# The last pair of a graph layer: inverse root on GpSimd, totals and turn-back in one PSUM slot, value copies on ScalarE

## The chip, the cores and the metric

The kernel runs on one core of a Trainium2 chip. The metric is the device time of one execution in microseconds (us); before the change three runs gave a median of 4974.71 us (4970.81 to 4975.93). In the profile PE is TensorE, DVE VectorE, ACT ScalarE, POOL GpSimd, SP the queue that issues all transfers. Everything is fp32, and each fp32 product shows as two matrix instructions in the trace (a transpose as one).

## What is computed

Two graph attention layers over 4096 nodes with 512 features and 8 heads of 64. Each normalizes its rows, takes the positive part, and adds attention to the input:

```python
h = jnp.maximum(_layernorm(x, axis=-1), 0.0)
x = x + _L0_gnn_ref(h, adj, L0_gnn_W, L0_gnn_b, L0_gnn_src_proj, L0_gnn_trg_proj)
h = jnp.maximum(_layernorm(x, axis=-1), 0.0)
x = x + _L1_gnn_ref(h, adj, L1_gnn_Wks, L1_gnn_Wqs, L1_gnn_Wvs, L1_gnn_Wo)

# layer 0, per head
e = src.T[:, :, None] + trg.T[:, None, :]
e = jnp.where(e >= 0, e, 0.01 * e) + connectivity[None, :, :]
out = jnp.einsum('hnm,hmd->hnd', jax.nn.softmax(e, axis=-1), data1.transpose(1, 0, 2))

# _layernorm
(x - m) / jnp.sqrt(v + eps)
```

Layer 1 needs keys, queries and values of the normalized output of layer 0 (`h @ Wks`, `h @ Wqs`, `h @ Wvs`).

## The kernel before

Layer 0 treats its four pairs of heads one after another. The first three take about 1715 us and are not touched. The fourth pair has a stage of its own (its pools are called `b0...`), in which the rows of layer 0 become complete, and which therefore also normalizes them and makes layer 1's keys, queries and values. Layer 1 follows from about 2530 us on and isn't touched.

**Tiling.** A row block is 128 rows, 32 of them in the stage (NG). A row block has four steps (GS): a step is 32 rows, laid on 128 partitions as four column ranges of 1024, for both heads. So the stage has 128 steps (SETS), and eight steps make a norm block of two row blocks (BR). All intermediate tiles of a row block stay in a ring of 12 slots (RING), that is three row blocks.

**Order.** The order is written out by hand in the loop at the end of the stage, under a manual schedule: each engine does what the loop records for it, in that order, and waits where a result or a buffer isn't there yet. In step s:

- SP: the mask loads for step s+3 (L586).
- ACT: for the first step of a row block, `out_of_psum` of the row block before (boT, L665); then `leaky` of step s+1 (two of 128x1024 into PSUM, L599), `exps` of step s-3 (two of 128x1024, L641). The two PSUM tiles `lk` are all there is, so `leaky` of step s+1 waits for `masked` of step s.
- DVE: `masked` of step s (two of 128x1024, L609, with the row's minimum), `squares` of step s-4 (a transpose in 32x32 squares, 128x2048, L648).
- POOL: at odd s `parted` (L616), the minima spread for a product.
- `work()`: up to six units of a projection job (below).
- At even s `smallest`: PE brings the minima of two steps together (nmB, L625), DVE takes them (L630); `exps` needs them.
- `endings`: one more piece of each running `finish` (below), the oldest first.
- PE: `weighted` of step s-8, a quarter of the products of a row block (32 instructions, L656). With the fourth quarter, a new `finish` begins.

**finish.** It is a generator that goes on by one piece per step. After the step with the fourth quarter, before the change: in the second step PE sums the totals (den, L672) and DVE takes their reciprocal (L676). In the fourth PE turns the attention back (back, L680), DVE divides (L682), POOL adds it to the rows (L686), SP writes them (L687). In the fifth DVE takes the moments (L690, L694). For the second row block of a norm block it goes on: in the sixth ACT takes the root (L700), in the seventh DVE the reciprocal (L702) and POOL normalizes both row blocks (L706), in the ninth and tenth PE transposes one of them each (tp, L716) and DVE takes the positive part out of PSUM (bhT, L717). Then a projection job is queued.

**Projection job.** 48 units per norm block: 32 for keys and queries in four tiles (mp, L727), each copied out by ACT (L733), and 16 for values in two tiles (mpv, L739), each copied out by DVE (L745). SP writes them to DRAM (L734, L746). Eight steps with six units are 48 units, so one job just fills the time until the next.

**PSUM slots.** Two slots with the tag `mp` are shared by mp, mpv and tp. One slot with the tag `ms` is shared by nmB, den and back. Root and exponential belong to different tables of ACT; the program loads a table where they alternate (the rows ACT_TABLE_LOAD).

Of the kernel before, what the change touches and what calls it, by code (L numbers as in the profile page):

```python
# [8 lines left out]
F32 = mybir.dt.float32  # L9
AF = mybir.ActivationFunctionType  # L10
ALU = mybir.AluOpType
# [4 lines left out]
P = 128  # L16
EPS = 1e-5
# [6 lines left out]
def kernel(  # L24
# [14 lines left out]
    nc = tc.nc  # L39
    N, DM = x.shape  # L40
    H, D = src_proj.shape[1:]
# [9 lines left out]
    const = ctx.enter_context(tc.tile_pool(name="const", bufs=1))  # L51
    dram = ctx.enter_context(tc.tile_pool(name="dram", bufs=1, space=DRAM))

    ident = const.tile([P, P], F32, name="ident")
    make_identity(nc, ident)
    eps = const.tile([P, 1], F32, name="eps")
    nc.gpsimd.memset(eps, EPS)


    SQ = 32  # L60
    NS = P // SQ
    band = const.tile([P, SQ], F32, name="band")
# [36 lines left out]
    with tc.tile_pool(name="a0k", bufs=1) as pk, tc.tile_pool(name="a0v", bufs=4) as pv, tc.tile_pool(  # L99
        name="a0a", bufs=3  # L100
    ) as pa, tc.tile_pool(name="a0t", bufs=6) as pt, tc.tile_pool(name="a0p", bufs=4) as pp, tc.tile_pool(
        name="a0x", bufs=1
    ) as px, tc.tile_pool(name="a0h", bufs=3) as ph, tc.tile_pool(name="a0s", bufs=4) as psb, tc.tile_pool(
        name="a0tr", bufs=3, space=PSUM
# [112 lines left out]
        def finish(G):  # L217

            rows, cols = bass.ts(G.g, P), bass.ts(G.c, PR)
            after = bass.ts(G.c + 1, PR)  # L220
            xt = px.tile([P, PR], F32, name="xt")
            nc.sync.dma_start(xt, x[rows, cols])
            oT = px.tile([P, P], F32, name="oT")
            nc.vector.tensor_copy(oT, G.o[:, :P])
            den = psb.tile([P, 2], F32, name="den")
            nc.vector.reciprocal(den, G.sm)
            yield
            back = G.o[:, P : 2 * P]
            nc.tensor.transpose(back, oT, ident)
            for i in range(len(G.blocks)):  # L230
                for kc in range(KC):
                    nc.tensor.matmul(
                        G.o[:, bass.ts(2 + i, P)], lhsT=G.hT[i][:, kc, :], rhs=wt[:, kc, after],
                        start=(kc == 0), stop=(kc == KC - 1),
                    )
            yield
            att = px.tile([P, 2, D], F32, name="att")
            nc.vector.tensor_mul(
                att, back.rearrange("p (h d) -> p h d", d=D), den.unsqueeze(2).to_broadcast([P, 2, D])
            )  # L240
            nc.gpsimd.tensor_add(xt, xt, att.rearrange("p h d -> p (h d)"))
            for i, b in enumerate(G.blocks):
                d1 = px.tile([P, PR], F32, name="d1")
                nc.vector.tensor_add(d1, G.o[:, bass.ts(2 + i, P)], bb[:, after])
                nc.sync.dma_start(d1_d[bass.ts(b, P), after], d1)
            nc.sync.dma_start(x1_d[rows, cols], xt)
# [178 lines left out]
        def step(n):  # L425
            return groups[n // 2], n % 2

        with tc.manual_schedule():
# [45 lines left out]
            for s in range(total + 6):  # L474
                G, h = step(s) if s < total else (None, 0)
                for half in range(2):
# [31 lines left out]
                    if 1 <= n <= 2 * total:  # L508
                        W, w = groups[(n - 1) // HALVES], (n - 1) % HALVES
                        weighted(W, w)  # L510
                        if w == 0:
                            load_rows_turned(W)
                        if W.g == NB - 1 and W.c + 1 < PAIRS:
                            load_feats(W.c + 1, w)
                        if w == HALVES - 1:
                            endings = [*endings[-1:], finish(W)]
# [12 lines left out]
    BR = 2  # L529
    UNITS = 6  # L530
    with tc.tile_pool(name="b0c", bufs=1) as pc, tc.tile_pool(name="b0a", bufs=4) as pa, tc.tile_pool(
        name="b0w", bufs=1
    ) as pk, tc.tile_pool(name="b0t", bufs=1) as pt, tc.tile_pool(name="b0v", bufs=GS) as pv, tc.tile_pool(
        name="b0x", bufs=6
    ) as pxr, tc.tile_pool(name="b0h", bufs=4) as ph, tc.tile_pool(name="b0e", bufs=4) as pe, tc.tile_pool(
        name="b0ht", bufs=2
    ) as phT, tc.tile_pool(
        name="b0s", bufs=6
    ) as psb, tc.tile_pool(name="b0o", bufs=1) as px, tc.tile_pool(
        name="b0lk", bufs=2, space=PSUM  # L540
    ) as plk, tc.tile_pool(name="b0m", bufs=1, space=PSUM) as pm, tc.tile_pool(
        name="b0po", bufs=1, space=PSUM
# [124 lines left out]
        def finish(G):  # L667

            yield
            den = pm.tile([P, P], F32, tag="ms", name="den")  # L670
            for k in range(GS):
                nc.tensor.matmul(  # L672
                    den[bass.ts(k, SQ), :2], lhsT=band, rhs=G.sm[:, k, :], start=True, stop=True
                )
            rden = psb.tile([P, 2], F32, name="rden")
            nc.vector.reciprocal(rden, den[:, :2])  # L676
            yield
            yield
            back = pm.tile([P, P], F32, tag="ms", name="back")
            nc.tensor.transpose(back, G.oT, ident)  # L680
            att = px.tile([P, 2, D], F32, name="batt")
            nc.vector.tensor_mul(  # L682
                att, back.rearrange("p (h d) -> p h d", d=D), rden.unsqueeze(2).to_broadcast([P, 2, D])
            )
            last = G.x[:, C3 * PR :]
            nc.gpsimd.tensor_add(last, last, att.rearrange("p h d -> p (h d)"))  # L686
            nc.sync.dma_start(x1_d[bass.ts(G.g, P), C3 * PR :], last)  # L687
            yield
            stats = psb.tile([P, 6], F32, name="bstats")
            nc.vector.bn_stats(stats, G.x)  # L690
            if G.g % BR == 0:
                block[0] = psb.tile([P, BR, 2], F32, name="bmv")
            mv = block[0]
            nc.vector.bn_aggr(mv[:, G.g % BR], stats)  # L694
            if G.g % BR < BR - 1:
                return
            Gs = groups[G.g - BR + 1 : G.g + 1]
            yield
            rstd = psb.tile([P, BR, 1], F32, name="brstd")
            nc.scalar.activation(rstd, mv[:, :, 1:2], AF.Sqrt, bias=eps)  # L700
            yield
            nc.vector.reciprocal(rstd, rstd)  # L702
            hns = []
            for j in range(BR):
                hn = ph.tile([P, DM], F32, name="bhn")
                nc.gpsimd.tensor_scalar(  # L706
                    hn, Gs[j].x, mv[:, j, 0:1], rstd[:, j], ALU.subtract, ALU.mult
                )
                hns.append(hn)
            yield  # L710
            hT = phT.tile([P, KC, BR * P], F32, name="bhT")
            for j in range(BR):
                yield
                tp = pmm.tile([P, KC, P], F32, tag="mp", name="tp")
                for kc in range(KC):
                    nc.tensor.transpose(tp[:, kc, :], hns[j][:, bass.ts(kc, P)], ident)  # L716
                nc.vector.tensor_scalar(hT[:, :, bass.ts(j, P)], tp, 0.0, None, ALU.max)  # L717
            jobs.append(projected(Gs, hT))

        def projected(Gs, hT):  # L720

            rows = bass.ts(Gs[0].g // BR, BR * P)
            for c in range(HC):
                mp = pmm.tile([P, 2, BR * P], F32, tag="mp", name="mp")
                for i, w in ((0, wk), (1, wq)):
                    for kc in range(KC):
                        nc.tensor.matmul(  # L727
                            mp[:, i], lhsT=w[:, kc, bass.ts(c, P)], rhs=hT[:, kc, :],
                            start=(kc == 0), stop=(kc == KC - 1),
                        )  # L730
                        if (i, kc) == (1, KC - 1):
                            e = pe.tile([P, 2, BR * P], F32, name="e")
                            nc.scalar.copy(e, mp)  # L733
                            nc.sync.dma_start(qk_d[:, c, :, rows], e)  # L734
                        yield 1
            for j in range(BR):
                mp = pmm.tile([P, 512], F32, tag="mp", name="mpv")
                for kc in range(KC):
                    nc.tensor.matmul(  # L739
                        mp, lhsT=hT[:, kc, bass.ts(j, P)], rhs=wv[:, kc, :],  # L740
                        start=(kc == 0), stop=(kc == KC - 1),
                    )
                    if kc == KC - 1:
                        e = pe.tile([P, 512], F32, name="e")
                        nc.vector.tensor_copy(e, mp)  # L745
                        nc.sync.dma_start(v_d[bass.ts(Gs[j].g, P), :], e)  # L746
                    yield 2

# [16 lines left out]
        with tc.manual_schedule():  # L765
# [4 lines left out]
            for s in range(SETS + PROD + 10):  # L770
# [23 lines left out]
                if s % 2 and s < SETS:  # L794
                    G, k = step(s)
# [3 lines left out]
                if s % 2 == 0 and 0 <= s - 2 < SETS:  # L799
                    G, k = step(s - 2)  # L800
# [3 lines left out]
                if 0 <= n < SETS:  # L804
                    W, w = step(n)
                    weighted(W, w)
                    if w == GS - 1:
                        endings = [*endings[-2:], finish(W)]
# [21 lines left out]
    with tc.tile_pool(name="a1t", bufs=1) as pt, tc.tile_pool(name="a1k", bufs=4) as pkk, tc.tile_pool(  # L830
        name="a1v", bufs=GS
    ) as pv, tc.tile_pool(name="a1a", bufs=6) as pa, tc.tile_pool(name="a1q", bufs=2) as pq, tc.tile_pool(
        name="a1x", bufs=2
    ) as px, tc.tile_pool(name="a1s", bufs=6) as psb, tc.tile_pool(name="a1z", bufs=2) as pz, tc.tile_pool(name="a1at", bufs=3) as pat, tc.tile_pool(
        name="a1sc", bufs=4, space=PSUM
    ) as psc, tc.tile_pool(name="a1tr", bufs=1, space=PSUM) as ptr, tc.tile_pool(
        name="a1m", bufs=2, space=PSUM
# [263 lines left out]
        with tc.manual_schedule():  # L1101
# [18 lines left out]
            for s in range(total + PROD + 3):  # L1120
# [16 lines left out]
                if s % 2 and 0 <= s - 3 < total:  # L1137
                    G, k = step(s - 3)
                    smallest(G, k // 2)
                n = s - PROD  # L1140
                if 0 < n <= total and n % GS == 0:
                    finish(groups[n // GS - 1])
# [12 lines left out]
                if s % 2 and s < total:  # L1155
                    G, k = step(s)
# [16 lines left out]
            for j in range(rb, NB):  # L1173
                projected(j)
# [28 lines left out]
```

## Time and profile before

| what | value |
|---|---|
| median of three runs | 4974.71 us (4970.81 to 4975.93) |
| profiled execution, its own time | 4974.76 us |
| its span, first to last instruction | 4973.0 us, mean clock 0.978 |
| busy: PE, DVE, ACT, POOL | 4747.3, 4509.1, 3912.2, 396.1 us |
| the last pair of layer 0 | about 1715 to 2530 us |
| ACT_TABLE_LOAD at L700 and L641 | 15 and 14, 1283 ns each |
| L700, root on ACT | 16, 296 ns each |
| L706, norm on POOL (subtract, multiply) | 32, 2073 ns each |
| L338, norm on POOL in an earlier stage (multiply, add) | 32, 768 ns each |
| L745, value copy on DVE | 32, 670 ns each |
| L733, key and query copy on ACT | 64, 566 ns each |

How to read it: a row names the line, the engine, the operation and the tiles (output <- input, partitions x elements). Matrix instructions are pipelined, so their mean is not their distance. The share of busy time is a mean over a stage; waits show who stood still for whom, and where a wait was for several things, the trace names the one that came last, which need not be the one that was late.

### The profile page before, as it was taken

How to read it: one execution, taken by the hardware profiler on the slowest of the kernel's cores; microseconds unless marked ns; L12 is line 12 of the kernel's file. 1: busy time of each engine (PE TensorE's matmuls, PEld its weight loads, DVE VectorE, ACT ScalarE, POOL GpSimd, SP SyncE). 2: the span in 40 equal slices, each digit the busy share in tenths (PEclk: the TensorE clock that was granted, in tenths of full speed). 3: DMA queues.
4: the chain of work that ended last, by engine and by line, in shares of the span. 5: the costliest groups of instructions: out<-in, count | busy, mean ns of one | idle time of the engine just before them, and what ended most of it. 6: DMA issues, size and time to landing. Idle time of an engine off the chain costs nothing.

```text
span 4973.0 us, 145263 instructions
## 1 busy us (share of the span) xinstructions
PE 4747.3 (95%) x61554; PEld 3507.7 (71%) x61554; DVE 4509.1 (91%) x7969; ACT 3912.2 (79%) x4557; POOL 396.1 (8%) x676
## 2 busy tenths in 40 slices
PE   6999999999999868998989999999999999999998
PEld 5888888888888756776746656666666666666664
DVE  4999999999999898888659999999999999999981
ACT  4999999999999898888658888666666666666660
POOL 1000000000000011111112222000000000000000
PEclk8999999999999979999999999999999999999999
DMA  6444454445444474444377787634444343533435
GB/s 236 156 150 162 171 183 154 157 154 197 165 147 163 121 170 141 134 143 141 100 217 242 239 261 239 200 129 144 137 160 152 128 153 127 187 128 136 152 121 191
DMA packets 358842, 819.49 MB, mean 165 GB/s; under 512 B 60080, under 2 KB 179120, under 8 KB 333104
## 3 DMA queue, kind: packets, MB, share of 16 engines
q1 hardware_dynamic: 358192, 810.21, 49.8%
q8 instruction: 483, 7.91, 0.7%
q14 instruction: 167, 1.37, 0.1%
HBM read 669.26 MB, written 140.77 MB: 163 GB/s over the span
## 4 chain that ended last, share of the span: by engine, by line
PE 42%; DMA 3%; issue 2%; SPq 1%; ACT 1%; DVE 1%; POOL 0%; ACTq 0%; POOLq 0%; DVEq 0%
PE sc L915 17%; PE o L996 17%; PE tr L979 5%; PE oo L1079 2%; DMA a<-in_adj_dram 2%; ACT t L966 1%; PE nmB L950 1%; SPq L889 1%; POOL a L902 0%; DVE t L931 0%; PE mp L727 0%; DMA z<-inv_d 0%; PE mpv L739 0%; DMA att_d<-z 0%; DMA v<-v_d 0%
## 5 line engine op out<-in xcount | busy, mean ns | idle before, releaser
L931 DVE CUSTOM_DVE_ANT_0 t<-sc,a 128x512 f32<-128x512 f32 x2048 | 1291.3, 686 | 70.8 <-issue 41.2
L966 ACT ACTIVATE t<-t,nm 128x1024 f32<-128x1024 f32 x1024 | 1168.0, 1143 | 177.3 <-DVE nm L955 177.3
L996 PEld LDWEIGHTS o<-t,v 128*64 128x64 f32 x16384 | 884.6, 137 | 428.7 <-issue 363.1
L915 PE MATMUL sc<-k,q 64*32 64x512 f32 x16384 | 1004.0, 597 | 10.6 <-DVE nm L931 10.5
L996 PE MATMUL o<-t,v 128*64 128x128 f32 x16384 | 1008.3, 276 | 0.0
L973 DVE STREAM_TRANSPOSE t<-t 128x1536 f32<-128x1536 f32 x512 | 907.7, 1773 | 5.0 <-ACT t L966 2.0
L158 DVE CUSTOM_DVE_ANT_0 t<-t,a 128x2048 f32<-128x2048 f32 x384 | 877.0, 2284 | 38.8 <-ACT t L147 38.7
L181 PE MATMUL tr<-ident,t 128*128 128x128 f32 x6144 | 781.4, 278 | 34.0 <-ACT pT L190 20.1
L203 PE MATMUL o<-pT,v 128*64 128x128 f32 x12288 | 756.9, 276 | 1.1 <-DVE pT L192 1.0
L181 PEld LDWEIGHTS tr<-ident,t 128*128 128x128 f32 x6144 | 665.4, 141 | 125.8 <-issue 65.3
L147 ACT ACTIVATE t<-tb,src 128x4096 f32<-128x4096 f32 x192 | 731.6, 3811 | 16.8 <-DMA tb<-trg_d 16.8
L168 ACT ACTIVATE t<-t,nm 128x4096 f32<-128x4096 f32 x192 | 731.2, 3808 | 8.6 <-DVE nm L163 8.5
L203 PEld LDWEIGHTS o<-pT,v 128*64 128x64 f32 x12288 | 664.1, 137 | 61.4 <-issue 47.4
L192 DVE COPY pT<-tr 128x1024 f32<-128x1024 f32 x549 | 653.6, 1216 | 9.8 <-PE tr L181 9.8
L985 ACT COPY t<-tr 128x512 f32<-128x512 f32 x512 | 298.9, 584 | 445.6 <-PE tr L979 441.8
L915 PEld LDWEIGHTS sc<-k,q 64*32 64x32 f32 x16384 | 251.3, 106 | 351.6 <-issue 314.4
L979 PE MATMUL tr<-ident,t 128*128 128x128 f32 x2048 | 348.5, 288 | 11.6 <-ACT t L966 8.4
L599 ACT ACTIVATE lk<-tb,srcb 128x1024 f32<-128x1024 f32 x256 | 282.3, 1113 | 82.3 <-DVE nm L609 75.2
L609 DVE CUSTOM_DVE_ANT_0 bt<-lk,ba 128x1024 f32<-128x1024 f32 x256 | 301.9, 1215 | 24.8 <-ACT e L733 12.7
L648 DVE STREAM_TRANSPOSE bt<-bt 128x2048 f32<-128x2048 f32 x128 | 295.1, 2306 | 28.9 <-ACT bt L641 28.9
L979 PEld LDWEIGHTS tr<-ident,t 128*128 128x128 f32 x2048 | 213.9, 141 | 116.1 <-issue 83.1
L641 ACT ACTIVATE bt<-bt,nm 128x1024 f32<-128x1024 f32 x256 | 290.3, 1135 | 0.4 <-DVE nm L630 0.3
(115 smaller groups left out, 3781.7 us busy)
## 6 DMA issues: line engine op xcount, KB each, us to landing
a<-in_adj_dram SPq DMA_DIRECT2D x192, 1024.0 KB
a<-pen_d SPq DMA_DIRECT2D x384, 512.0 KB
ba<-in_adj_dram SPq DMA_DIRECT2D x512, 128.0 KB
a<-in_adj_dram SPq DMA_DIRECT2D x512, 128.0 KB
pen_d<-a SPq DMA_DIRECT2D x128, 512.0 KB
h<-hT_d SPq DMA_DIRECT2D x96, 256.0 KB
qk_d<-e SPq DMA_DIRECT2D x64, 256.0 KB
x<-in_x_dram SPq DMA_DIRECT2D x8, 1024.0 KB
```

The source lines that it names most:

```text
L147: nc.scalar.activation(t, targets[G.c, h], AF.Prelu, bias=src[:, G.g, 2 * G.c + h : 2 * G.c + h + 1], alpha=SLOPE)
L158: nc.vector.tensor_tensor_reduce(out=t, in0=t, in1=rows_of_adj[G, f], scale=-1.0, scalar=FMAX, op0=ALU.add, op1=ALU.min, accum_out=nm[:, f ...
L168: nc.scalar.activation(G.t[h], G.t[h], AF.Exp, bias=G.nm[h][:, NCH : NCH + 1], scale=-1.0, accum_out=G.sm[:, h : h + 1],)
L181: nc.tensor.transpose(tr[:, bass.ts(b % 4 * 2 + h, P)], G.t[h][:, bass.ts(i * MB + b, P)], ident)
L192: nc.vector.tensor_copy(pT, tr)
L203: nc.tensor.matmul(G.o[h * D : (h + 1) * D, :P], lhsT=feats[G.c][i][:, b, bass.ts(h, D)], rhs=pT[:, bass.ts(b % 4 * 2 + h, P)], start=(mb ...
L915: nc.tensor.matmul(sc[h][bass.ts(a, SQ), :], lhsT=G.q[bass.ts(h, D), bass.ds(G.q0 + k * SQ, SQ)], rhs=keys[G.c][half][bass.ts(h, D), a, :] ...
L931: nc.vector.tensor_tensor_reduce(out=t[:, G.ring + k, h, cols], in0=scs[half][h], in1=a[:, cols], scale=1.0, scalar=FMAX, op0=ALU.add, op1 ...
L966: nc.scalar.activation(u, u, AF.Exp, bias=G.nm[k // 2][:, k % 2, h : h + 1], scale=-1.0, accum_out=G.sm[:, h, k : k + 1],)
L973: nc.vector.transpose(u, u)
L979: nc.tensor.transpose(tr[:, bass.ts(h * NT + m, P)], t[:, G.ring + k, h, bass.ds(VC + m * P, P)], ident)
L996: nc.tensor.matmul(G.o[bass.ts(h, D), :P], lhsT=v[:, b, bass.ts(h, D)], rhs=t[:, bass.ds(G.ring, GS), h, bass.ds(at, SQ)], start=(mb == 0) ...
```

## The change

In the stage of the last pair:

- ACT's root and DVE's reciprocal are replaced by POOL: add epsilon, raise to the power -0.5, multiply by the mean, negate. The norm itself becomes a multiply-add with two values per row.
- The totals and the turn-back of a row block share one tile in the `ms` slot, and are done in the same piece of `finish`; the pieces after it follow sooner, so that a job is queued seven steps after the fourth quarter instead of ten.
- The value copies go from DVE to ACT, where they follow `exps` of the step.

Line numbers after the first edit are two higher in the changed kernel, and others shift by a few more.

```diff
+    neghalf = const.tile([P, 1], F32, name="neghalf")
+    nc.gpsimd.memset(neghalf, -0.5)
...
         def finish(G):
 
             yield
-            den = pm.tile([P, P], F32, tag="ms", name="den")
+            ms = pm.tile([P, 2, P], F32, tag="ms", name="back")
             for k in range(GS):
                 nc.tensor.matmul(
-                    den[bass.ts(k, SQ), :2], lhsT=band, rhs=G.sm[:, k, :], start=True, stop=True
-                )
+                    ms[bass.ts(k, SQ), 1, :2], lhsT=band, rhs=G.sm[:, k, :], start=True, stop=True
+                )
+            nc.tensor.transpose(ms[:, 0], G.oT, ident)
             rden = psb.tile([P, 2], F32, name="rden")
-            nc.vector.reciprocal(rden, den[:, :2])
-            yield
-            yield
-            back = pm.tile([P, P], F32, tag="ms", name="back")
-            nc.tensor.transpose(back, G.oT, ident)
+            nc.vector.reciprocal(rden, ms[:, 1, :2])
             att = px.tile([P, 2, D], F32, name="batt")
             nc.vector.tensor_mul(
-                att, back.rearrange("p (h d) -> p h d", d=D), rden.unsqueeze(2).to_broadcast([P, 2, D])
+                att, ms[:, 0].rearrange("p (h d) -> p h d", d=D), rden.unsqueeze(2).to_broadcast([P, 2, D])
             )
...
             if G.g % BR < BR - 1:
                 return
             Gs = groups[G.g - BR + 1 : G.g + 1]
-            yield
+
             rstd = psb.tile([P, BR, 1], F32, name="brstd")
-            nc.scalar.activation(rstd, mv[:, :, 1:2], AF.Sqrt, bias=eps)
-            yield
-            nc.vector.reciprocal(rstd, rstd)
+            nc.gpsimd.tensor_scalar(rstd, mv[:, :, 1:2], 1.0, EPS, ALU.mult, ALU.add)
+            nc.gpsimd.tensor_tensor(rstd, rstd, neghalf.unsqueeze(1).to_broadcast([P, BR, 1]), ALU.pow)
+            shift = psb.tile([P, BR, 1], F32, name="bshift")
+            nc.gpsimd.tensor_mul(shift, mv[:, :, 0:1], rstd)
+            nc.gpsimd.tensor_scalar(shift, shift, -1.0, 0.0, ALU.mult, ALU.add)
             hns = []
             for j in range(BR):
                 hn = ph.tile([P, DM], F32, name="bhn")
-                nc.gpsimd.tensor_scalar(
-                    hn, Gs[j].x, mv[:, j, 0:1], rstd[:, j], ALU.subtract, ALU.mult
-                )
+                nc.gpsimd.tensor_scalar(hn, Gs[j].x, rstd[:, j], shift[:, j], ALU.mult, ALU.add)
                 hns.append(hn)
+            yield
             yield
...
                     if kc == KC - 1:
                         e = pe.tile([P, 512], F32, name="e")
-                        nc.vector.tensor_copy(e, mp)
+                        nc.scalar.copy(e, mp)
                         nc.sync.dma_start(v_d[bass.ts(Gs[j].g, P), :], e)
```

## Prediction

> **What bounds the kernel now.** I first cut the span into stretches. Layer 0's last pair, the only stage that the diff touches, runs from about 1715 to 2530 us; the rest of the 4973.0 us keeps its code. Its two parts, with busy time per engine (PE, weight loads, DVE, ACT, POOL):
>
> ```profile
> core 0: us, PE busy (x) PEld busy (x) DVE busy (x) ACT busy (x) POOL busy (x), PEclk, DMA share, GB/s
> 1870.00:2437.00 567.00, 515.27 (x4486) 403.42 (x4485) 501.10 (x693) 498.18 (x697) 75.18 (x100) 0.93 0.47 136
> 2437.00:2530.00 93.00, 89.84 (x598) 64.35 (x604) 24.50 (x42) 17.17 (x30) 10.70 (x9) 1.00 0.30 104
> ```
>
> In the loop PE, DVE and ACT are all near 90%: none is the bound alone, they wait for each other. The ending is PE alone. The waits from 1870 to 2430 us say where (total, times, longest):
>
> ```profile
> ACT lk L599 <- DVE nm L609: 65.7, 48, 2.3
> PEld mpv L739 <- ACT e L733: 45.7, 12, 3.8
> DVE bt L648 <- ACT bt L641: 25.2, 12, 2.1
> PE tp L716 <- DVE e L745: 15.1, 12, 1.6
> DVE bhT L717 <- PE tp L716: 13.5, 12, 1.1
> DVE bt L609 <- ACT e L733: 12.7, 8, 1.6
> ```
>
> Twelve times means once per norm block, that is two row blocks, eight steps. I number the steps 0 to 7 (s modulo 8). The time line of one block (start, duration) shows the episode at its step 0:
>
> ```profile
> 2060.08 2.31 DVE L648 STREAM_TRANSPOSE bt<-bt 128x2048 f32<-128x2048 f32 x1 [2.10 <-ACT bt L641]
> 2062.49 1.21 DVE L609 CUSTOM_DVE_ANT_0 bt<-lk,ba 128x1024 f32<-128x1024 f32 x1
> 2064.30 0.56 ACT L733 COPY e<-mp 128x512 f32<-128x512 f32 x1
> 2064.91 1.12 PE L739 MATMUL mpv<-wv,bhT 128*128 128x512 f32 x2 [2.98 <-DVE nm L609]
> 2067.00 0.65 DVE L745 COPY e<-mpv 128x512 f32<-128x512 f32 x1
> 2067.71 1.12 PE L716 MATMUL tp<-ident,bhn 128*128 128x128 f32 x4 [1.49 <-DVE e L745]
> 2068.76 3.68 PE L656 MATMUL bo<-bt,bv 128*64 128x128 f32 x32
> 2068.87 0.69 DVE L717 TENSOR_SCALAR bhT<-tp 128x512 f32<-128x512 f32 x1 [1.13 <-PE tp L716]
> ```
>
> ACT's copy at 2064.30 is late because two table loads ran ahead of it. PE waits 2.98 us for its slot (the releaser named, a DVE instruction, was long done; the weight load's line names ACT's copy), then 1.49 us for DVE's value copy. Then PE is slow: its 32 products take 3.68 us against 1.97 elsewhere. It ends the block late, and the mask of step 4, which needs PE's last products (ring slot), waits 1.6 us.
>
> [...] L338, the multiply-add that the new line copies, takes 768 (page, group L338), against 2073 for L706.
>
> **The change, part by part.** I use start-to-start times of this time line: DVE two masks 2.28, turn 2.24, minimum .06, bhT .60, moments .97, reciprocal and att .25 to .30; ACT two leaky 2.16 to 2.20, two exps 2.27, copy .50 (.56 to its end), boT .16; PE six work units 2.70, nmB .22, den and back .3, 32 products 1.90, tp .53 (readable after .69 to .81). Walking the old order with these, from step 1 on, gives the starts of the traced block within .05 us, so I trust the same walk for the new order.
>
> *Root on POOL.* Removes per block two loads and Sqrt from ACT (2 x 1.28 + .3 = 2.9 us) and a reciprocal from DVE (.07). In the built order 30 loads go: 15 at L700, 14 at L641, one at L966. POOL gets four small operations: three like L616 (.22, with hops about 1.0 us together) and a power that no row shows. Lower bound: .22, it can't be less than the copy-sized L616 and gains nothing. Upper bound: none in the trace. Cover: POOL starts at 14.9 (moments of step 2), adds 1.0 and two norms of .77, ends at 17.4; behind it `parted` of step 3 must be done by 21.7, when PE comes to nmB of step 4. So 4.0 us are free; beyond that PE pays one for one. I take .3, nothing. The norms as multiply-add save POOL 2 x 1.3 us per block; POOL is busy 75 of 567 us, so nothing. The constant's memset (L57's like took 98 ns) comes before any load has landed: nothing. L966's load (1283 ns) stands in a stretch in which layer 1 waits for its first transfers: nothing; uncovered it would be 1.3.
>
> *One slot, earlier chain.* Den, back, att, x1 write move two steps earlier or none, moments two, job three. The back-transpose waits for boT, done seven us before. POOL's add and SP's x1 write move along; behind the write SP has the next mask loads, three steps ahead (14 us), so nothing. Queueing a job three steps earlier puts 18 of 48 work units before the ending: 18 x .44 = 7.9 us of PE less there, where PE is the bound (89.84 of 93). This is the surest gain; I take 8.
>
> *Value copies.* 24 copies of .6 us net leave DVE in this window, .5 come to ACT. But ACT's copy stands behind leaky and exps of its step. The second transposes take a slot that is free, the first (tp0, step 5 now) needs mpv0's copy. So a chain: mask h0, leaky, exps, copy, tp0, bhT, and bhT stands before the next mask on DVE; on PE the next products stand behind tp0.
>
> Two more waits come with them. At the copy ACT can wait for PE, with the next leaky queued behind: in the walk mpv1 is ready at 38.1, exps end at 38.5, so it doesn't, and the leaky behind waits for its mask until 41.9 anyway, 3 us of cover. SP's value write waits some 1.4 us longer for ACT than for DVE; behind it stand mask loads that are wanted three steps later: nothing.
>
> *The walk.* (A mask of step 0 or 4 also waits for PE's last products of the row block three before, whose ring slot it takes; a step's products follow its work; leaky of the next step follows a step's first mask by 1.27.) Masks start at 0, 4.57, 9.31, 14.85, 19.42, 23.99; PE's work at -.2, 4.63, 9.60, 14.42, 19.02, 23.84; leaky at 1.27, 6.20, 11.09, 16.12, 20.73, 25.62. The wait for the projections' copy is gone: it ends at 25.72, PE wants it at 25.7. In step 5 DVE is free at 28.50, PE at 26.8; ACT ends exps at 25.62 + 2.16 + 2.27 = 30.05, copy at 30.61, tp0 starts 30.67. PE has idled 3.9 us, longer than the 2.98 that slows it today. With 4 us at half clock (today 5.0 in one block, 3.2 in another): bhT at 31.83, mask 6 at 32.80, PE's work 35.35, nmB 38.35, bhT 39.06, moments, mask 7 at 40.63; PE's products of step 7 start at 43.4 and free the ring 2.09 later: the next block at **45.5**. The end matches the assumed start (PE .2 ahead), so it repeats.
>
> Before, steps 24 to 128 take 1834.1 to 2436.4, 602.3 us, 13 blocks of 46.3. After: 13 x 45.5 = 591.5, and .5 for the first moments moved ahead of step 24: -10.3. With the ending: -18.3. The profiled execution took 4974.76 (span 4973.0 and 1.8 around), .05 from the median: **4956.5**.
>
> **Rivals.**
> 1. *PE stays at full clock* through the gap [...]. Then mask 6 at 32.2, work 33.6, mask 7 at 38.9, block 43.7: 13 x 43.74 + .5 = 569.1, -33.2, -8: 4933.6. [...] Against: 3.9 us is long.
> 2. *The gap eats the loop's gain.* Half clock lasts 1.6 us longer, into step 6; at half speed PE loses .8 more, once for itself and it moves mask 7 and the ring wait with it: block 46.3, loop 46.3 x 13 + .5 = 602.4, only the ending remains: 4974.76 + .1 - 8 = 4966.9. For: one traced block was slow for 5 us after its gap.
> 3. *POOL's power is slow* (slower than before). At 8 us it holds `parted` of step 3 by 4 us, nmB, minimum and exps follow: 13 x 4 = 52, less 18: 5008. It decides from 4 us on, and exceeds the old time from about 5.4. For: nothing shows the operation. Against: two elements per partition.
> 4. That it doesn't remove the loads: excluded by the built order.
>
> **How the numbers follow.** About 0.2% (10 us) is what a measurement can tell. Forecast 0.58 (faster), rival 1 0.15 (faster), rival 2 0.20 (0.02 of it faster, the rest same), rival 3 0.07 (0.06 slower, 0.01 same). Sums: faster 0.75, same 0.19, slower 0.06. Likeliest alone 4948 to 4963; the range 4936 to 4969 leaves out half of rival 1 and rival 3.
>
> **What would show it.** Right: no ACT_TABLE_LOAD after layer 0's first; PE's wait for the projections' copy gone; one wait per block of tp for ACT's value copy, 3 to 4 us, and of bhT for tp, about 3 us; ending from the last mask some 8 us shorter; L707 at 0.77. Wrong: masks waiting elsewhere than at steps 5 and 0; a power above 4 us; copies on ACT waiting for PE, which would hold leaky; a block shorter than 43.7 or longer than 47.

## The result, and the profile after

The changed kernel takes 4961.69 us (median of 14 runs, 4960.02 to 4965.1), beside 4974.39 for the kernel before (14 runs, 4970.74 to 4976.78): a ratio of 0.9976, with a 95% interval of 0.9968 to 0.9985. That is 12.7 us less, where 18.3 less had been forecast. The span of the profiled execution fell by 12.4, from 4973.0 to 4960.6.

The windows of the changed kernel, cut as those of before (busy PE, weight loads, DVE, ACT, POOL):

```profile
core 0: us, PE busy (x) PEld busy (x) DVE busy (x) ACT busy (x) POOL busy (x), PEclk, DMA share, GB/s
1870.00:2437.00 567.00, 522.65 (x4566) 406.18 (x4563) 498.34 (x663) 474.01 (x687) 55.26 (x146) 0.94 0.47 137
```

Against the same stretch of before, ACT has 24 us less, POOL 20 less and DVE 3 less. PE shows only 80 matrix instructions more: the loop is hardly faster. Its waits from 1870 to 2430 us (total, times, longest):

```profile
ACT lk L601 <- DVE nm L611: 85.7, 49, 3.6
PEld tp L716 <- ACT e L745: 54.3, 12, 4.5
PE tp L716 <- ACT e L745: 44.3, 12, 3.7
DVE bhT L717 <- PE tp L716: 39.7, 25, 3.2
DVE nm L632 <- PE nmB L627: 19.4, 13, 2.1
PEld mpv L739 <- ACT e L733: 8.4, 12, 0.7
```

The weight load's wait for the projections' copy (L733) fell from 45.7 us to 8.4. The wait of tp for the value copy (L745) rose from 15.1 us (for DVE) to 44.3 (for ACT), again twelve times, once per norm block. One wait took the place of the other. The time line of one block shows the chain at step 5 (start, duration):

```profile
2092.24 2.15 ACT L601 ACTIVATE lk<-tb,srcb 128x1024 f32<-128x1024 f32 x2
2094.33 1.14 ACT L643 ACTIVATE bt<-bt,nm 128x1024 f32<-128x1024 f32 x1
2095.46 1.14 ACT L643 ACTIVATE bt<-bt,nm 128x1024 f32<-128x1024 f32 x1
2096.59 0.57 ACT L745 COPY e<-mpv 128x512 f32<-128x512 f32 x1
2097.21 0.66 PE L716 MATMUL tp<-ident,bhn 128*128 128x128 f32 x4 [3.69 <-ACT e L745]
2097.91 0.69 DVE L717 TENSOR_SCALAR bhT<-tp 128x512 f32<-128x512 f32 x1 [2.70 <-PE tp L716]
2098.42 3.32 PE L658 MATMUL bo<-bt,bv 128*64 128x128 f32 x32
```

mpv0 was ready long before, but its copy stands behind two leaky and two exps. PE idles 3.69 us; its 32 products then take 3.32 us, elsewhere 1.97. In the next block the same stretch is slower still, and the half clock reaches into the work units (2.84 us for the same six in the block above):

```profile
2142.55 1.11 PE L716 MATMUL tp<-ident,bhn 128*128 128x128 f32 x4 [3.69 <-ACT e L745]
...
2144.22 3.68 PE L658 MATMUL bo<-bt,bv 128*64 128x128 f32 x32
2147.83 3.41 PE L739 MATMUL mpv<-wv,bhT 128*128 128x512 f32 x6
```

The groups of the new operations, same stretch (busy, mean ns):

```profile
L707 POOL TENSOR_SCALAR bhn<-xr,brstd,bshift 128x512 f32<-128x512 f32 x24 | 18.4, 773 | 1.3
L745 ACT COPY e<-mpv 128x512 f32<-128x512 f32 x25 | 14.3, 572 | 4.2 <-ACT bt L643 4.1
L700 POOL TENSOR_TENSOR brstd<-brstd,neghalf 128x2 f32<-128x2 f32 x12 | 8.4, 701 | 1.0
```

The power takes 0.70 us, the norm 0.77 in place of 2.07. Of table loads the profile has two left, L327 and L170, in layer 0's first stages.

**Where the 12.4 us come from.** I read the start of the first mask of step 24 and of step 120 (twelve blocks apart) from DVE's time line, and cut the span there:

| us | until step 24 | twelve blocks | from step 120 to the end of the span |
|---|---|---|---|
| before | 1834.11 | 555.03 | 2583.86 |
| after | 1836.76 | 551.46 | 2572.38 |
| difference | +2.65 | -3.57 | -11.48 |
| of it within the stage (its first mask to the last product of mpv) | +2.15 | -3.57 | -10.31 |
| forecast for the same cut | +0.5 | -9.0 | -9.8 |

The row for the stage leaves out +0.5 us ahead of it and -1.2 behind it, in code that both kernels share. The forecast row is the prediction's own: 12 x 45.5 is 546.0, and the last block (47.28 before, as I extrapolate it from the cycle of blocks) and the ending give -1.8 - 8. Within the stage the end gave 0.5 more than foreseen, and start and loop gave 7.1 less. The new blocks alternate between about 45.3 and 46.7 us.

### The profile page after: what moved, and what is told of

The parts are those of the page before. It is cut to its first block, busy times and chain, and to the rows that moved or that the text cites. A ratio compares the mean times of both kernels' runs of the same rounds, so it can differ in the third digit from the quotient of the medians.

```text
span 4960.6 us, 145294 instructions
## 1 busy us (share of the span) xinstructions
PE 4742.7 (96%) x61554; PEld 3495.5 (70%) x61554; DVE 4493.7 (91%) x7921; ACT 3882.2 (78%) x4543; POOL 376.2 (8%) x741
## 4 chain that ended last, share of the span: by engine, by line
PE 59%; ACT 15%; DVE 11%; issue 8%; DMA 5%; SPq 1%; POOL 0%; ACTq 0%; DVEq 0%; POOLq 0%
PE sc L915 17%; PE o L996 17%; PE tr L979 5%; ACT t L170 5%; DVE t L160 5%; PE mp L727 4%; DVE pT L194 4%; PE bo L658 4%; ACT t L149 3%; PE tr L183 3%; PE o L205 3%; ACT pT L192 2%; PE oo L1079 2%; DMA a<-in_adj_dram 2%; ACT bt L643 2%
## 5 line engine op out<-in xcount | busy, mean ns | idle before, releaser
L170 ACT ACTIVATE t<-t,nm 128x4096 f32<-128x4096 f32 x192 | 732.5, 3815 | 8.2 <-DVE nm L165 8.1
```

The costliest lines, as they stand in the source:

```text
L170: nc.scalar.activation(G.t[h], G.t[h], AF.Exp, bias=G.nm[h][:, NCH : NCH + 1], scale=-1.0, accum_out=G.sm[:, h : h + 1],)
```

## The experiments

My theory at this point: (1) the value copy's place behind the exps on ACT holds tp0, PE's gap halves its clock, and the long half clock is why a block takes 46.05 us on average (the last eight full blocks; over the twelve it is 45.96) and not 45.5; (2) the removed table loads are worth far more than the whole change, and the copies spend most of it; (3) the shorter chain is a gain of 8 us in the ending. Rivals: the copies are a gain because they relieve DVE; the late tp0 costs, not the clock; copies on ACT cost wherever they stand. "The kernel before" was measured anew with each set of four (medians 4975.27, 4975.5, 4973.53), and the ratios are to these; these medians differ by up to 2 us, so a difference between runs of two sets can be off by as much.

**One part at a time.** First the change without its third part:

```diff
-                        nc.scalar.copy(e, mp)
+                        nc.vector.tensor_copy(e, mp)
```

> The changed kernel with its two value copies per block back on VectorE; the rest of the change stays. Theory (the copy behind ScalarE's exps is what holds tp0, and the long gap halves PE's clock): VectorE copies mpv0 right after its turn of step 5, so tp0 starts some 1.4 us earlier than now, PE's gap falls from 3.7 to about 2.3 us, the half clock is shorter or gone, a block takes 44 to 45 us in place of 46.05 (mean of 12), and the time is 10 to 27 us below the changed kernel: 4935 to 4952. Rival (the copies' move was a gain, because VectorE is nearly full): 24 copies of 0.6 us come back into the loop, 14 us slower than the changed kernel, 4976. Rival (the gap does not matter, the blocks are held elsewhere): within 4 us of 4962.

Measured: 4932.05 us, ratio 0.9913 (0.9900 to 0.9927). That is 29.6 less than the changed kernel, 3 us below the theory's range, and both rivals are out. tp0's gap is 2.3 us, a block takes 43.7 on average.

Then the copies alone, on the kernel before:

```diff
-                        nc.vector.tensor_copy(e, mp)
+                        nc.scalar.copy(e, mp)
```

> The kernel before with only the value copies moved to ScalarE. There the copy of mpv0 falls in step 0 behind the copy of the projections, which already stands behind the exps and two table loads. Theory: tp0's wait is about what it was (ScalarE is just free), VectorE is 0.65 us freer twice per block, the block is still set by the late copy: within 5 us of the kernel before, 4970 to 4979. Rival (relief of VectorE is a gain by itself): 14 us faster, 4960. Rival (the move costs by itself, wherever the copies stand): 8 us or more slower.

Measured: 4998.35 us, ratio 1.0045 (1.0033 to 1.0058), 23 us slower. My theory missed it: I took ACT to be free when mpv0 is ready. The number is that of the last rival, a cost wherever the copies stand; only a run that changes their place can refute it (below). The time line shows that ACT isn't free: mpv0's last products start at 2076.66, its copy stands behind two leaky and two exps, and PE waits again.

```profile
2076.67 2.15 ACT L599 ACTIVATE lk<-tb,srcb 128x1024 f32<-128x1024 f32 x2
...
2081.02 0.56 ACT L745 COPY e<-mpv 128x512 f32<-128x512 f32 x1
2081.63 1.11 PE L716 MATMUL tp<-ident,bhn 128*128 128x128 f32 x4 [3.73 <-ACT e L745]
```

Before, this wait was 1.49 us. The copies alone cost about what they cost on top of the rest.

Then the root alone, on the kernel before (each step of the chain keeps its place):

```diff
             yield
             rstd = psb.tile([P, BR, 1], F32, name="brstd")
-            nc.scalar.activation(rstd, mv[:, :, 1:2], AF.Sqrt, bias=eps)
+            nc.gpsimd.tensor_scalar(rstd, mv[:, :, 1:2], 1.0, EPS, ALU.mult, ALU.add)
+            nc.gpsimd.tensor_tensor(rstd, rstd, neghalf.unsqueeze(1).to_broadcast([P, BR, 1]), ALU.pow)
...
             yield
-            nc.vector.reciprocal(rstd, rstd)
...
+                nc.gpsimd.tensor_scalar(hn, Gs[j].x, rstd[:, j], shift[:, j], ALU.mult, ALU.add)
```

> The kernel before with only the root on GpSimd and the norm as multiply-add; every step keeps its place, the value copies stay on VectorE. Theory: the two table loads per block go, the wait of 2.98 us for the projections' copy with them, PE stays at full clock, and a block takes about 44 us in place of 46.65: 12 x 2.6 = 31 us faster, 4943; the ending is as before. This would say that the loads' removal was worth far more than the whole change, and that the copies' gap spends it. Rival (the loop is held by VectorE and ScalarE, not by this wait): less than 8 us faster, 4966 or more.

Measured: 4933.21 us, ratio 0.9914 (0.9901 to 0.9928): 42 less, more than I had set. The steady block falls from 46.65 us (mean of a cycle of 45.9, 46.8 and 47.3) to about 43.4. By steps, 2.2 of the 3.3 us lie between step 7 and the next step 0 (6.87 before, 4.69 here). There DVE's turn waited 2.1 us for the exps that the table loads had held up, 25.2 us in twelve waits; here that row is gone. PE does not stay at full clock, as I had expected: from 1870 to 2430 us the granted clock is 0.97, against 0.93 before.

And the slot with the shorter chain alone:

```diff
-            den = pm.tile([P, P], F32, tag="ms", name="den")
+            ms = pm.tile([P, 2, P], F32, tag="ms", name="back")
...
-            yield
-            yield
-            back = pm.tile([P, P], F32, tag="ms", name="back")
-            nc.tensor.transpose(back, G.oT, ident)
...
                 hns.append(hn)
-            yield
```

> The kernel before with only the one slot for totals and turn-back and the chain three steps shorter (tp0 in step 5); the square root with its table loads stays on ScalarE, the value copies on VectorE. Theory: the ending loses 18 of its work units, 8 to 9 us; the loop keeps its table loads and about its length, for they now hold another copy: within 5 us. So 4966, between 4961 and 4971. Rival (the earlier chain costs in the loop what it saves in the ending): 4974 within 3 us.

Measured: 4973.22 us, ratio 0.9995 (0.9986 to 1.0003): the rival. What it gains and pays shows in the same cut, of the stage alone. Here the slot is added to three kernels:

| slot and shorter chain added to | steps 0 to 24 | twelve blocks | from step 120 on | stage |
|---|---|---|---|---|
| the kernel before | +3.09 | +4.95 | -9.34 | -1.3 |
| root on GpSimd alone | +4.15 | +3.27 | -9.42 | -2.0 |
| root, copies on ACT ahead of exps (e11 to e8, below) | +3.16 | +3.35 | -8.82 | -2.3 |

The ending's gain is about as forecast, 8.8 to 9.4 us. But the 18 work units that leave it must be done three steps earlier from the first block on, and steps 0 to 24 take 3.1 to 4.2 us longer in all three. In the kernel before, the block of steps 24 to 31 took 42.78 us, since it was not yet full of them; with the shorter chain it is nearly full (45.96 in this run). In the other two kernels that block explains little (+0.4 and -1.8 us): the ones after it take 0.3 to 0.5 us more each, and why is not shown. Start and blocks together pay 6.5 to 8 us of the gain back.

**Which copy.** Only mpv0's copy back on DVE:

```diff
-                        nc.scalar.copy(e, mp)
+                        (nc.scalar.copy if j else nc.vector.tensor_copy)(e, mp)
```

> The changed kernel with only the first value copy of a block (mpv0's, the one that tp0 waits for) on VectorE and the second on ScalarE. Theory (only the copy ahead of tp0 matters): like both copies on VectorE, 4932 within 4 us; perhaps a little less, since VectorE has 0.65 us less per block. Rival (each value copy on ScalarE costs): halfway back, 4947 within 4 us.

Measured: 4932.76 us, ratio 0.9914 (0.9900 to 0.9927), the same as with both on DVE. So mpv1's copy costs nothing on either engine; all of the 29 us hang on the one that tp0 waits for.

**Clock or lateness.** Fillers ahead of tp0, six in the changed kernel and four with both copies on DVE; they add work whose result nobody reads:

```diff
                 yield
+                if j == 0:
+                    fill = pm.tile([P, 512], F32, tag="ms", name="fill")
+                    for i in range(6):
+                        nc.tensor.matmul(fill, lhsT=ident, rhs=wv[:, i % KC, :], start=True, stop=True)
                 tp = pmm.tile([P, KC, P], F32, tag="mp", name="tp")
```

> The changed kernel, copies on ScalarE, with six matmuls of 512 columns whose result nobody reads (2.99 us at full clock by L739's six) in PE's gap ahead of tp0: nothing comes earlier, PE is only kept busy. Theory (of the block's 46.05 us a good part is the half clock that follows the gap): PE stays at full clock, tp0, the 32 products and the work units of steps 5 and 6 run at full speed, and a block takes the 43.7 us of the walk with a warm PE: 13 x 2.35 = 31 us faster than the changed kernel, 4931. Rival (what costs is the late tp0 and bhT behind it, not the clock): 4962 within 4 us, or slower by the fillers.

> Both value copies on VectorE and four such fillers (2.0 us) in the remaining gap of 2.3 us. Theory: most blocks there (44.05 us) still carry some half clock, every fifth (42.42) none; with fillers all are like the fifth: 10 of 13 blocks x 1.6 = 16 us faster than without fillers, 4916. Rival (the blocks' difference has another cause): 4932 within 4 us.

Measured: 4960.75 us, ratio 0.9970 (0.9959 to 0.9982), and 4934.73, ratio 0.9918 (0.9904 to 0.9931). Both near their rivals, but neither decides: I had sized the fillers wrongly. One fp32 product is two matrix instructions in the trace, so L739's six are three products, and a filler takes 0.88 us. Six took 5.31 us and held tp0 themselves, by 1.3 us (7.89 us after the first mask of step 5, 6.59 in the changed kernel); four, 3.5 us in a gap of 2.3, did much the same. In both runs all full blocks are alike (45.03 and 43.32 us). I repeated it with four in the changed kernel:

```diff
-                    for i in range(6):
+                    for i in range(4):
```

> The changed kernel with four fillers of 512 columns ahead of tp0. In the run with six, one filler took 0.88 us (5.31 for six, not the 0.50 that I took it for), so six ran 1.5 us past the copy that tp0 waits for and held tp0 themselves; four take 3.54 us and fit the gap of 3.7. Theory (half clock is a large share of the block): the block is that with six fillers less what they ran over, 45.03 - 1.5 = 43.5, close to the walk's 43.7 for a warm PE; 12 to 13 blocks x 2.5 = 30 us faster than the changed kernel, 4928 to 4937. Rival (the late tp0 is the cost): 4960 within 4 us.

Measured: 4939.01 us, ratio 0.9930 (0.9916 to 0.9943), 22.7 us below the changed kernel, just outside the range set: the twelve blocks gain 26.0, and from step 120 on 3.6 are lost, since the fillers run in the ending too. Its time line on PE:

```profile
2126.60 3.60 PE L717 MATMUL fill<-wv,ident 128*128 128x512 f32 x8
2130.46 0.66 PE L720 MATMUL tp<-ident,bhn 128*128 128x128 f32 x4 [0.26 <-ACT e L749]
2131.04 0.24 PE L674 MATMUL back<-bsm,band 128*32 128x2 f32 x8
2131.22 0.33 PE L677 MATMUL back<-ident,boT 128*128 128x128 f32 x1
2131.48 1.97 PE L658 MATMUL bo<-bt,bv 128*64 128x128 f32 x32
```

tp0 waits for the same copy and comes no earlier, but the 32 products take 1.97 us, and the granted clock from 1870 to 2430 us is 1.00, against 0.94 without them. All full blocks take 43.79 us; the walk had 43.7 for a PE at full clock. So of the changed kernel's 46.05 us, 2.26 are half clock. Lateness costs less: with both copies on DVE four blocks of five take some 44.0 us and one takes 42.42. That this one holds no half clock is an estimate (3.41 us of it in each of the others make a granted clock of 0.97 from 1870 to 2430 us, and 0.97 was measured); then lateness costs 1.37 per block at most.

**Place or engine.** The changed kernel with `work()` moved ahead of the exps in the loop; both copies stay on ACT:

```diff
+                work()
                 if 0 <= s - EXPS < SETS:
                     exps(*step(s - EXPS))
...
-                work()
```

> The changed kernel with the step's work units written ahead of its exps: both value copies stay on ScalarE but stand ahead of the two exps, not behind them; PE's and VectorE's order is the same. Theory (the copy's place in ScalarE's queue is the cause, not the engine): tp0 starts 2 us earlier than in the changed kernel, PE's gap is about 1.7 us, and the time is at or below that with both copies on VectorE: 4920 to 4938. Rival (a copy on ScalarE costs wherever it stands, because ScalarE has no room): 4955 or more.

Measured: 4912.35 us, ratio 0.9872 (0.9857 to 0.9888), 49 us below the changed kernel and below the range set. Place, not engine. The copies of keys and queries move ahead of the exps too, and their share of the gain was not told apart; in the changed kernel only the weight load still waited for them, 8.4 us in all. tp0's gap is 1.60 us; two blocks of three take 41.55 us, the third 43.18. The same with one filler:

> The kernel with the work units ahead of the exps (4912) and one filler (0.88 us) in its remaining gap of 1.6 us. There two blocks of three take 41.55 us and every third 43.18. Theory (the third has a half clock that the gap starts): all take 41.55, 4 x 1.6 = 6 us faster, 4906. Rival: 4912 within 3 us.

Measured: 4904.76 us, ratio 0.9863 (0.9849 to 0.9876). All full blocks take 41.55 us. This is the fastest version found; of its lead over the version without a filler the block lengths leave no doubt, while the intervals of the two ratios overlap.

**Two more undone parts.** The slot and the shorter chain taken out of the early-copy kernel (totals, turn-back and the chain's steps as before):

> The kernel with root on GpSimd, value copies on ScalarE and the work units ahead of the exps, but with totals and turn-back in slots of their own and the chain three steps longer, as before. Theory (a shorter chain only moves 18 work units from the ending into a loop that pays for them just as much): within 4 us of the same kernel with the one slot, 4912. Rival (the prediction's own step: the ending gets 8 us shorter and nothing is paid elsewhere): 4920.

Measured: 4913.1 us, ratio 0.9878 (0.9865 to 0.9892), within 1 us: the shorter chain gives nothing that the times can tell here either.

And the kernel before with the exps written behind the work units:

```diff
-                if 0 <= s - EXPS < SETS:
-                    exps(*step(s - EXPS))
...
                 work()
+                if 0 <= s - EXPS < SETS:
+                    exps(*step(s - EXPS))
```

> The kernel before with one thing changed: exps are written behind the step's work units, so that ScalarE's copy of the projections stands ahead of the exps and of the table load that these need. Nothing of the change is in it; square root and all table loads stay. Theory (PE's wait for that copy, and the half clock behind it, is the loop's cost): the copy comes about 3.5 us earlier, the wait of 2.98 us is gone, a block takes some 44 us in place of 46.65: 25 to 35 us faster than the kernel before, 4940 to 4950. Rival (it is the table loads' own 2.6 us per block on a full ScalarE): less than 8 us faster, 4967 or more.

Measured: 4975.55 us, ratio 1.0005 (0.9997 to 1.0013): my theory of the old kernel fell. The projections' copy does come earlier, and PE's wait for it shrinks from 2.98 us to 0.74, but the next wait grows to fill the place:

```profile
2065.39 1.12 PE L739 MATMUL mpv<-wv,bhT 128*128 128x512 f32 x2 [0.74 <-ACT e L733]
...
2067.64 2.31 DVE L648 STREAM_TRANSPOSE bt<-bt 128x2048 f32<-128x2048 f32 x1
...
2069.88 0.65 DVE L745 COPY e<-mpv 128x512 f32<-128x512 f32 x1
...
2070.58 1.11 PE L716 MATMUL tp<-ident,bhn 128*128 128x128 f32 x4 [3.94 <-DVE e L745]
```

DVE's value copy stands behind masks and turn of the step, 4.66 us after the first mask (4.51 in the kernel before). So the wait that the prediction put first, PE's for the projections' copy, hid the one behind it, and its end alone gains nothing. DVE's wait for the exps at its turn stays here (25.4 us in twelve waits), and went with the loads in the run of the root alone. This points to the late turn as what the table loads cost; no run took that wait away alone.

## Why the forecast held, and where it was off

- *Direction and place.* Held: faster, no table load left in the stage, PE's wait for the projections' copy gone, one wait of 3.69 us of tp for ACT's copy per block, bhT behind it, half clock after it. The walk gave 8.81 us from step 5 to step 6 and 7.83 to step 7; the trace has 8.36 and 7.75 in a short block, about 8.8 and 8.7 in a long one. One step of it failed without a cost: mpv1 was to be ready before the exps end, but in the six long blocks ACT waited 0.4 to 0.8 us for it (4.1 us in all; in one the exps end at 2150.60, mpv1's products at 2151.24, the copy starts at 2151.32). The leaky behind it still waited 2.8 us for its mask, as the prediction's cover had it.
- *Root on POOL.* Held: no stall of nmB for `parted`. The four small operations take 0.19 + 0.70 + 0.20 + 0.19 = 1.28 us where 1.0 was taken with 0.3 for the power; the slack of 4.0 covers it. Loads and norm were priced only inside the walk. By itself this part is worth 42 us (34.9 in the twelve blocks), and nowhere did the prediction say so.
- *Value copies.* The chain was right and the slot's wait too. What was not seen is its price: 25 to 28 us over twelve blocks (alone and on top of the rest), three quarters of what the root brings. The net of the two, -9 us in the forecast, is a small difference of large numbers.
- *Half clock: the mis-sized term.* "With 4 us at half clock" put the block at 45.5. The clock records of the trace have 3.41 us of it in every short block and 6.83 in every long one, 5.1 on average; the 1.1 more than taken, at half speed, are some 0.56 us per block (an estimate), about the excess of 46.05 over 45.5. The prediction's reading of the kernel before, 5.0 and 3.2, was short as well: eleven of its twelve blocks hold 6.6 to 6.8. The short blocks lose about 1.4 us to it in step 5's 32 products (3.32 against 1.97), the long ones 2.8 (tp 0.5, products 1.7, work 0.6). Six long blocks are 6.5 us above the forecast in all, six short ones 1.0 below: these are the 5.5 us that the twelve blocks lack. Rival 2, the gap eats the loop's gain, is thus true of every second block. Rival 1's walk, 43.7 with PE at full clock, is what the four fillers gave (43.79). That the 4 us came this near is in part luck: nothing in the prediction decides between no half clock, 3.41 us of it and 6.83 (below).
- *One slot, earlier chain.* "This is the surest gain; I take 8." The step that failed as reasoning: the ending did get shorter (8.8 to 9.4 us where the slot is added alone), but the prediction held the price at the start at +0.5. Within the stage, steps 0 to 24 take 2.15 us longer, and 3.1 to 4.2 where the slot is added alone. The first block of the twelve, 42.78 us before, takes 46.08; this price stands in the sum unseen, for 13 x 45.5 counts every block as full, against a measured 602.3 in which one was not and the steady block took 46.65, not 46.3. The end was forecast well, the price ahead of step 24 was left out, and alone the step is worth 1.3 to 2.3 us of the stage.
- *The sum.* Off by 5.9 us in the span: +1.65 at the start, +5.4 in the blocks, -0.5 at the end, -0.7 outside the stage.

The granted clock itself is in the traces. In the profiles of the two kernels, before and after, every stretch of one granted clock between the first and the last that were recorded lasts a whole multiple of 3.413 us, and the shortest lasts just that. The blocks of a kernel repeat in a pattern. Where it is fixed, its length too is near a whole multiple of 3.413 us:

| kernel | blocks in the pattern | its length, us | / 3.413 |
|---|---|---|---|
| before | 3 | 139.94 | 41.0 |
| after | 2 | 92.14 | 27.0 |
| copies only | 4 | 194.56 | 57.0 |
| slot only | 3 | 139.99 | 41.0 |
| copies back on DVE | 5 | 218.48 | 64.0 |
| early copy | 3 | 126.28 | 37.0 |

Root alone keeps no fixed pattern: three of its blocks are 130.06 us, 38.1 times 3.413, and its short blocks follow each other after three blocks and then after four. Where the fillers fit the gap there is no pattern: 43.79 and 41.55 us in every full block, 12.83 and 12.17 times 3.413. That the steps of the clock decide which blocks are long is an estimate of mine from these lengths; no run shows it by itself.

In the changed kernel a short and a long block have 40.96 us at full clock, 3.41 at half, 40.96 at full and 6.83 at half: 92.16 in all, where the two blocks take 92.14. Cut into stretches of 3.41 us at the changes of the clock, the two blocks shown above read (PE's busy time, granted clock):

```profile
core 0: us, PE busy (x), PEclk, DMA share, GB/s
2094.41:2097.82 3.41, 0.61 (x8) 1.00 0.43 123
2097.82:2101.23 3.41, 3.41 (x36) 0.50 0.34 112
2138.78:2142.19 3.41, 0.08 (x1) 1.00 0.69 215
2142.19:2145.61 3.42, 3.06 (x27) 0.50 0.22 81
2145.61:2149.02 3.41, 3.41 (x24) 0.50 0.60 175
2149.02:2152.43 3.41, 3.41 (x24) 1.00 0.01 2
```

A gap of the same length was followed by slow products in one place and not in another. In one block of the early-copy kernel PE idles 1.60 us ahead of tp0, and its 32 products, from 2160.02 us on, take 3.28 us; in another it idles 1.59, and the products, from 2118.47 on, take 1.97. What sets the two apart was not shown: no run shifted the phase or varied the gap alone.

## What to carry to other kernels

Before moving a small copy to an engine with room, look at what stands ahead of it in that engine's queue at the moment when its source is ready, and who waits for the buffer that it frees: 0.57 us of ACT behind 4.35 us of other work cost 28 us, and with the step's copies ahead of the exps the same engine was 20 us faster than DVE had been with its copies in their old place. Where a change shortens a chain in a loop that is full, the work that leaves the ending appears at the start; cut the span in three before counting the gain. And where PE waits in short gaps (1.6 to 3.7 us here), price the clock after the gap apart from the gap, and try a filler: it is cheap, and tells the two apart.

## What the runs showed of the hardware

- A power by a tensor of exponents on POOL takes 0.70 us for 128x2, against 0.19 for a multiply-add or 0.20 for a product of the same size.
- Useless matrix work gained time: 3.6 us of it per block took 22.7 us off the changed kernel; the granted clock from 1870 to 2430 us was 1.00 with it and 0.94 without.
- In the profiles before and after, stretches of one granted clock between the first and the last were whole multiples of 3.413 us. In the changed kernel half clock began within 1.8 us of the end of the gap of 3.7 us on PE in all twelve blocks, and lasted 3.41 us in six and 6.83 in six. In the early-copy kernel the 32 products behind a gap of 1.6 us took 3.28 us in one block and 1.97 in another.
